# Own semaphores for the row gathers, one wait of TensorE for five rows, and buffers filled in alternating direction, in a relational graph layer

## The chip, the cores and the metric

The kernel runs on one core of a Trainium2 chip. The metric is the device time of one execution in microseconds. Three runs of the kernel before took 18,929.84, 18,938.22 and 18,953.83 us, so the median is 18,938.22 us. Lower is better.

Five engines with an instruction stream of their own take part: TensorE (PE: products, and PEld: its weight loads), VectorE (DVE), ScalarE (ACT), GpSimd (POOL) and SyncE (SP, which only issues transfers). They order their work by semaphores: an instruction can wait until a semaphore has reached a value, and can step one when it is done.

## The reference, cut to what matters

Two relational graph layers over 50,000 nodes with 128 features and 850,000 edges of 16 relations, with 8 basis matrices, then a residual and a layer norm:

```python
def _rgcn_layer(h, src, dst, rel, basis, w_comp, loop_w, bias):
    W = jnp.einsum('rb,bio->rio', w_comp, basis)
    seg = dst.astype(jnp.int32) * N_REL + rel.astype(jnp.int32)
    agg = jax.ops.segment_sum(h[src], seg, num_segments=N_ENT * N_REL)
    agg = agg.reshape(N_ENT, N_REL, -1)
    msg = jnp.einsum('nri,rio->no', agg, W)
    out = msg + h @ loop_w + bias
    return jax.nn.relu(out)

h = _rgcn_layer(x, src, dst, rel_type, basis1, w_comp1, loop_w1, bias1)
h = _rgcn_layer(h, src, dst, rel_type, basis2, w_comp2, loop_w2, bias2)
x = _layernorm(x + h, axis=-1)
```

The edges come sorted by their target `dst`. 50,000 of them are loops of a node to itself, and the kernel handles those apart; 800,000 remain.

## The kernel before

**Chunks.** The 800,000 edges are cut into rows of 128 edges, and ten rows (`K = 10`) are a chunk: 625 chunks (`C`) for each of the two layers `n`, 1,250 in all, run through by `for c in range(C)`. The two halves of a chunk have five rows each (`PER = 5`).

**Gathers.** For each row of a chunk one gather (`gather`, L198, an indirect DMA issued by GpSimd) fetches the 128 source nodes' features, 512 bytes each, from `x` or, in the second layer, from `H1`. The ten rows of a chunk land in one of six buffers (`rows[(n * C + c) % GATHERS]`, tile `g`, `GATHERS = 6`), row `k` in `g[:, k, :]`. The program text issues the gathers of chunk `c + 2` in round `c` (`FETCH = 2`). GpSimd has a stream of its own, and does nothing else in the loop but ten scatters to `FULL` (L372) and ten to `LREL` (L428) in the first layer, so it runs on ahead until a buffer is not free.

**Products of a chunk on TensorE.** For each row `k`, `pa` (L837) multiplies the gathered rows by `hot`, a matrix of 128 edges x 96 (8 bases x 12 target slots) that VectorE makes (L789) from the edges' relation weights `pm` (L615, five products for each four chunks) and their slots `own` (L782). Five products fill one bank of `pa`; then ScalarE copies it into `aT` (L844), twice for each chunk. In the next round eight products over the bases (`slots`, L689) add up `ps`, which ScalarE copies to `slots` (L693); one round later `nodes_of` spreads the slots onto nodes (`pn`, L703 and L707), adds the part of the loops (L709), applies the relu and stores `H1`, or the norm and the output.

**Loops.** `from_itself` handles the nodes' own edges, 391 tiles of 128 nodes for each layer, 0.63 for each chunk: a transpose on TensorE (L205) with its copy (L207), two products with four bases each (`hb`, L667) that VectorE weighs into `by` (L670), one with the loop matrix (L678, taken over at L679), a sum (L681) and a store to `L`.

**Order.** The instructions of TensorE and GpSimd stay in the order of the text (`manual_schedule` for these two engines); a chunk's own blocks are interleaved with steps of the generators `parts`. The other engines are put in order by the scheduler.

**Waits.** The framework adds the waits. Software-issued DMAs take eight semaphore lanes in turn, so gather `i` waits until gather `i - 8`, the last one on its lane, has landed. Each gather waits as well for the product that read its row six chunks earlier, and each of the ten products waits for its own row's lane. Every one of the ten products steps TensorE's semaphore, by one. A product steps it by more where earlier ones in the group have no step of their own: the eight products of L689 by eight at the last, the five of L615 by five.

Of the kernel before, what the change touches and what calls it, by code (L numbers as in the profile page):

```python
# [53 lines left out]
K = P // WN  # L54
# [10 lines left out]
PER = 5  # L65
Q = AT // 2
GATHERS = 6
# [9 lines left out]
def tile_rgcn_resnorm(  # L77
# [15 lines left out]
    nc = tc.nc  # L93
# [4 lines left out]
    C = -(-M // (K * P))  # L98
# [5 lines left out]
    def needed(j):  # L104

        end = min(2 * C, ROWS[j + 1] if j + 1 < len(ROWS) else 2 * C) * LIVE
        return min(NG - 1, -(-(end + LIVE) * E // (M * RUN * P)) - 1) if j else 0
# [87 lines left out]
    ps_h = ctx.enter_context(tc.tile_pool(name="ps_h", bufs=1, space=PSUM))  # L195

    def gather(to, of, idx):
        nc.gpsimd.indirect_dma_start(  # L198
            out=to, out_offset=None, in_=of, in_offset=bass.IndirectOffsetOnAxis(ap=idx, axis=0)
        )  # L200

# [13 lines left out]
    rows = [consts.tile([P, K, D], F32, name=f"g{i}") for i in range(GATHERS)]  # L215
    src = consts.tile([P, 2 * C * HALF], I32, name="src")
# [366 lines left out]
    def chunked():  # L583
        with (
# [5 lines left out]
            def at(c):  # L590
                return nc.values_load(
                    base_i[0:1, c : c + 1],
                    engines=[mybir.EngineType.SP],
                    min_val=0,
                    max_val=N - P,
                    skip_runtime_bounds_check_because="bases are clamped to N - P, and no node is below 0",
                )
# [129 lines left out]
            def asked(c):  # L727

                return min(NT, -(-(c + 1) * NT // C) + AHEAD)

            def asked_by(c):

                return min(NT, -(-asked(c) // AT) * AT) * P
# [21 lines left out]
            def later_rows():  # L755
                g = 0
                for j in range(1, len(ROWS)):
                    while g < needed(j):
                        g += 1
                        yield from runs(g, pr, lambda: asked_by(min(C - 1, now[0] + 2)))  # L760
                    yield from rows_of(j, pr)
                    ready[0] = j
                while g < NG - 1:
                    g += 1
                    yield from runs(g, pr, lambda: asked_by(min(C - 1, now[0] + 2)))

            coming = later_rows()
            ordered = ExitStack()
            ordered.enter_context(tc.manual_schedule(engines={mybir.EngineType.PE, mybir.EngineType.Pool}))
            for n, of in enumerate((x, H1)):  # L770

                kept, summed_up, multiplied, lws = None, None, None, []
                base, ks = [at(0), None, None], lambda c: min(K, -(-M // P) - c * K)
                own_parts = []

                def own_nodes(c):

                    return range(asked(c - 1) if c > 1 else 0, asked(c) if c else 0)

                def hot_of(c, pm):  # L780
                    own = hp.tile([P, K, WN], F32, name="own")
                    nc.vector.tensor_tensor(  # L782
                        own[:, : ks(c)],
                        grid[:, None, :WN].to_broadcast([P, ks(c), WN]),
                        key[:, c * K : c * K + ks(c), None].to_broadcast([P, ks(c), WN]),
                        op=OP.is_equal,
                    )
                    hot = hp.tile([P, K, NB, WN], F32, name="hot")
                    nc.vector.tensor_tensor(  # L789
                        hot[:, : ks(c)],  # L790
                        pm[:, c % Q * K : c % Q * K + ks(c), :, None].to_broadcast([P, ks(c), NB, WN]),
                        own[:, : ks(c), None, :].to_broadcast([P, ks(c), NB, WN]),
                        op=OP.mult,
                    )
                    return hot

                def loaded(n0):

                    ls = sb.tile([P, D], F32, name="ls_of")
                    nc.sync.dma_start(ls, L[n][ds(n0, P), :])  # L800
                    xw = None
                    if n:
                        xw = sb.tile([P, D], F32, name="xw")
                        nc.sync.dma_start(xw, x[ds(n0, P), :])
                    return ls, xw

                weigh = weights(0, n)
                next(weigh)
                for c in range(C):
                    now[0] = c  # L810
                    if n == 0 and c:

                        next(coming, None)
                        while ready[0] + 1 < len(ROWS) and 2 * min(C, c + FETCH + 4) > ROWS[ready[0] + 1]:
                            next(coming)
                    if c:
                        base = [at(c)] + base[:2]
                    for to in range(0 if c == 0 else c + FETCH, min(C, c + FETCH + 1)):
                        for k in range(ks(to)):
                            gather(rows[(n * C + to) % GATHERS][:, k, :], of, src[:, to * K + k : to * K + k + 1])  # L820
                    g = rows[(n * C + c) % GATHERS]
                    if c == 0:
                        if n == 0:
                            done(first_runs)
                        pm = next(weigh)
                        hot = hot_of(c, pm)
                    if c > 1:
                        kept = nodes_of(kept, c - 2, ks(c - 2), summed_up, base[2], *others, n)
                        others = loaded(base[1])
                    parts = own_parts[0] if own_parts else iter(())  # L830
                    next(parts, None)
                    aT = hp.tile([P, NB, S], F32, name="aT")
                    for k in range(0, ks(c), PER):
                        m = min(PER, ks(c) - k)
                        pa = ps_a.tile([P, BANK], F32, name="pa")
                        for i in range(m):
                            nc.tensor.matmul(  # L837
                                pa[:, i * NB * WN : (i + 1) * NB * WN],
                                g[:, k + i, :],
                                hot[:, k + i].rearrange("e b w -> e (b w)"),  # L840
                                start=True,
                                stop=True,
                            )
                        nc.scalar.copy(  # L844
                            aT[:, :, k * WN : (k + m) * WN].rearrange("d b (i w) -> d i b w", w=WN),
                            pa[:, : m * NB * WN].rearrange("d (i b w) -> d i b w", i=m, w=WN),
                        )
                        if k == 0:
                            next(parts, None)
                            if c:  # L850
                                summed_up = slots(c - 1, ks(c - 1), multiplied, n)
                            next(parts, None)
                    multiplied = aT
                    for parts in own_parts:
                        done(parts)
                    if c == 1:
                        others = loaded(base[1])
                    if c + 1 < C:
                        if (c + 1) % Q == 0:
                            pm = next(weigh)  # L860
                        hot = hot_of(c + 1, pm)
                        if c + 2 < C and (c + 2) % Q == 0:
                            weigh = weights(c + 2, n)
                            next(weigh)
                        own_parts = []
                        for i in own_nodes(c + 1):
                            own_parts.append(from_itself(i, of, n, lws))
                            if len(own_parts) == 1:
                                next(own_parts[0])
                    if n == 0 and c == 3:  # L870
                        beginning.close()
                    if n == 0 and c == C - 1:
                        done(coming)
                        count_up(pr)
                last = loaded(base[0])
                kept = nodes_of(kept, C - 2, ks(C - 2), summed_up, base[1], *others, n)
                summed_up = slots(C - 1, ks(C - 1), multiplied, n)
                nodes_of(kept, C - 1, ks(C - 1), summed_up, base[0], *last, n)
# [189 lines left out]
```

## Time and profile before

| | |
|---|---|
| median of three runs | 18,938.22 us |
| profiled execution, its own time | 18,936.72 us |
| its span, first to last instruction | 18,934.8 us |
| mean granted clock of TensorE | 0.720 of full speed |
| busy: TensorE products, weight loads | 10,703.0 us, 9,174.1 us |
| busy: GpSimd | 11,864.7 us |
| busy: VectorE, ScalarE | 6,595.5 us, 2,775.4 us |
| transfers | 1,227 MB, mean 65 GB/s |
| gathers (L198) | 12,500, some 947 ns each |
| products of L837 | 12,500, two records each (f32) |

How to read it: PE is recorded in two records for each f32 product, with PEld beside it. A line of a group names the line of the kernel, the engine, the operation, out<-in by tile names, and the count, then the busy time and the mean in ns, then the engine's idle time just before and what ended most of it. "remote" and "another core or an unknown queue" mean that the profile found no instruction that could have ended the wait. "issue" is time in which the engine waited for nothing that the profile shows. The ends of TensorE's records are modelled by the profiler, not observed. A gather's record ends when its transfer has been issued, not when the rows have landed.

### The profile page before, as it was taken

Reading aid. Unit: us, or ns where it says so; the run is one execution under the profiler, and the core shown is the slowest. Engines: PE = TensorE matmul, PEld = TensorE weight load, DVE = VectorE, ACT = ScalarE, POOL = GpSimd, SP = SyncE. Lnnn points to the kernel's source line nnn. Section 1 sums busy time; section 2 is a strip of 40 time slices with the busy share of each in tenths; the row PEclk is TensorE's granted clock in tenths of the full one; section 3 lists DMA queues with packets and bytes.
Section 4 is the critical chain, followed back from the end, with each engine's and each line's share of the span. In section 5 each row is a group of like instructions: output and inputs, shape, how many; then the busy total and the mean of one; then the engine's idle time right before and its main releaser. Section 6 shows DMA issues by size and latency. Waiting matters only on the chain.

```text
span 18934.8 us, 187693 instructions
## 1 busy us (share of the span) xinstructions
PE 10703.0 (57%) x59198; PEld 9174.1 (48%) x59198; DVE 6595.5 (35%) x14269; ACT 2775.4 (15%) x7815; POOL 11864.7 (63%) x12533
## 2 busy tenths in 40 slices
PE   4555555555555555555555555555555555555555
PEld 3444445444544445445445555445454444444445
DVE  4333334333333332333223333333333333333333
ACT  1111111111111111111111111111111111111111
POOL 5666666665666666666656666666666666666665
PEclk7777777676777776777767777777777777777777
DMA  2222222222222222222222222222222222222222
GB/s 80 69 69 65 68 66 66 66 66 63 62 62 61 61 61 61 61 61 61 61 55 66 67 66 67 66 66 67 65 66 66 66 66 66 65 66 66 66 65 62
DMA packets 1164943, 1227.02 MB, mean 65 GB/s; under 512 B 283055, under 2 KB 952401, under 8 KB 1163937
## 3 DMA queue, kind: packets, MB, share of 16 engines
q0 software_dynamic: 403552, 826.82, 16.8%
q1 hardware_dynamic: 757169, 386.65, 7.1%
q8 instruction: 472, 7.73, 0.2%
q14 instruction: 534, 4.37, 0.1%
q10 hardware_dynamic: 3216, 1.45, 0.0%
HBM read 1059.55 MB, written 154.23 MB: 64 GB/s over the span
## 4 chain that ended last, share of the span: by engine, by line
another core or an unknown queue 22%; PE 17%; issue 7%; DVE 5%; ACT 2%; DMA 0%; POOL 0%; SPq 0%; ACTq 0%; DVEq 0%; POOLq 0%
PE pa L837 6%; PE ps L689 4%; PE hb L667 4%; DVE ls L681 1%; DVE by L670 1%; DVE hot L789 1%; PE pn L703 1%; ACT aT L844 1%; PE pn L707 1%; PE po L678 0%; PE po L205 0%; DVE by L679 0%; ACT slots L693 0%; ACT sd L574 0%
## 5 line engine op out<-in xcount | busy, mean ns | idle before, releaser
L198 POOL DMA_INDIRECT g<-H,src x6250 | 5910.6, 946 | 3393.7 <-issue 1422.2
L198 POOL DMA_INDIRECT g<-in_x_dram,src x6250 | 5927.4, 948 | 3338.4 <-issue 1411.5
L837 PE MATMUL pa<-hot,g 128*128 128x96 f32 x25000 | 4125.3, 326 | 1898.8 <-DVE hot L789 1388.2
L837 PEld LDWEIGHTS pa<-hot,g 128*128 128x128 f32 x25000 | 4014.2, 243 | 2402.1 <-DVE hot L789 1434.6
L689 PEld LDWEIGHTS ps<-basis,aT 128*120 128x120 f32 x20000 | 3222.4, 240 | 927.1 <-issue 849.3
L667 PE MATMUL hb<-basis,hT 128*128 128x512 f32 x3128 | 2273.3, 818 | 2107.1 <-ACT hT L207 915.7
L689 PE MATMUL ps<-basis,aT 128*120 128x128 f32 x20000 | 3211.3, 329 | 224.3 <-issue 150.5
L670 DVE TENSOR_TENSOR by<-hb,lw 128x512 f32<-128x512 f32 x1564 | 1080.1, 691 | 6152.1 <-remote 2557.6
L789 DVE TENSOR_TENSOR hot<-pm,own 128x960 f32<-128x960 f32 x1250 | 1432.6, 1153 | 4113.1 <-remote 3585.2
L844 ACT COPY aT<-pa 128x480 f32<-128x480 f32 x2500 | 1395.2, 558 | 6619.3 <-remote 3577.7
L703 PE MATMUL pn<-slots,own 120*128 120x128 f32 x2500 | 708.5, 373 | 2448.5 <-ACT slots L693 1502.1
L703 PEld LDWEIGHTS pn<-slots,own 120*128 120x128 f32 x2500 | 470.3, 235 | 2593.2 <-ACT slots L693 1583.3
L667 PEld LDWEIGHTS hb<-basis,hT 128*128 128x128 f32 x3128 | 638.1, 253 | 2191.4 <-ACT hT L207 943.1
L681 DVE TENSOR_REDUCE ls<-by 128x128 f32<-128x1152 f32 (+1 forms) x782 | 1656.9, 2119 | 12.1
L693 ACT COPY slots<-ps 120x128 f32<-120x128 f32 x1250 | 332.4, 266 | 5771.4 <-remote 3733.1
L205 PE MATMUL po<-ident,h_own 128*128 128x128 f32 (+1 forms) x782 | 295.8, 378 | 1151.9 <-issue 399.5
L205 PEld LDWEIGHTS po<-ident,h_own 128*128 128x128 f32 (+1 forms) x782 | 138.1, 177 | 1219.9 <-issue 415.1
L707 PE MATMUL pn<-kept,shift 128*128 128x128 f32 x2496 | 604.8, 332 | 12.1 <-DVE shift L706 6.3
L615 PE MATMUL pm<-each,is_rel 128*128 128x64 f32 x3140 | 438.6, 281 | 114.4 <-issue 110.4
L707 PEld LDWEIGHTS pn<-kept,shift 128*128 128x128 f32 x2496 | 493.7, 245 | 14.2 <-DVE shift L706 7.7
L712 ACT COPY kept<-pn 128x128 f32<-128x128 f32 x1248 | 336.1, 269 | 1079.7 <-DVE a L709 603.5
L709 DVE TENSOR_TENSOR a<-pn,ls_of 128x128 f32<-128x128 f32 x1250 | 355.1, 284 | 386.6 <-remote 133.1
(148 smaller groups left out, 5082.0 us busy)
## 6 DMA issues: line engine op xcount, KB each, us to landing
g<-in_x_dram,src POOLq DMA_INDIRECT x6250
g<-H,src POOLq DMA_INDIRECT x6250
ls_of<-L SPq DMA_DIRECT2D x1250, 64.0 KB
L<-ls SPq DMA_DIRECT2D x780, 64.0 KB
H<-h SPq DMA_DIRECT2D x625, 64.0 KB
xw<-in_x_dram SPq DMA_DIRECT2D x625, 64.0 KB
out_dram<-o SPq DMA_DIRECT2D x625, 64.0 KB
h_own<-in_x_dram SPq DMA_DIRECT2D x390, 64.0 KB
```

What stands on the lines that cost most here:

```text
L198: nc.gpsimd.indirect_dma_start(out=to, out_offset=None, in_=of, in_offset=bass.IndirectOffsetOnAxis(ap=idx, axis=0))
L205: nc.tensor.transpose(tp[:, :m], h, ident[:m, :m])
L615: nc.tensor.matmul(of[:, :, j * NB : (j + 1) * NB], is_rel[:m, j * P : (j + 1) * P], EACH[n][:m], start=True, stop=True,)
L667: nc.tensor.matmul(hb[:m], hT, BASIS[n][:, b : b + few, :].rearrange("p b d -> p (b d)"), start=True, stop=True)
L670: nc.vector.tensor_tensor(by[:m, b : b + few, :], hb[:m].rearrange("p (b d) -> p b d", d=D), lw[:m, b : b + few, None].to_broadcast([m, fe ...
L681: nc.vector.tensor_reduce(ls[:m], by[:m].rearrange("p b d -> p d b"), AX.X, OP.add)
L689: nc.tensor.matmul(ps[: k * WN], aT[:, b, : k * WN], BASIS[n][:, b, :], start=b == 0, stop=b == NB - 1)
L703: nc.tensor.matmul(pn, own[: k * WN], st[: k * WN], start=True, stop=not c)
L707: nc.tensor.matmul(pn, shift, kept, start=False, stop=True)
L789: nc.vector.tensor_tensor(hot[:, : ks(c)], pm[:, c % Q * K : c % Q * K + ks(c), :, None].to_broadcast([P, ks(c), NB, WN]), own[:, : ks(c), ...
L837: nc.tensor.matmul(pa[:, i * NB * WN : (i + 1) * NB * WN], g[:, k + i, :], hot[:, k + i].rearrange("e b w -> e (b w)"), start=True, stop=True,
L844: nc.scalar.copy(aT[:, :, k * WN : (k + m) * WN].rearrange("d b (i w) -> d i b w", w=WN), pa[:, : m * NB * WN].rearrange("d (i b w) -> d i ...
```

## The change

Each half of each of the six buffers gets a semaphore of its own, `landed[0]` to `landed[11]`. Every gather steps the one of its half by 16 when it lands, instead of a lane, and the framework is told to leave these gathers' completion to it. Of a half's five products only the first waits, for the count that stands for all five rows; the others are declared free of it. A buffer is filled from row 0 to 9 in one use and from 9 to 0 in the next (`in_turn`), and the halves and rows are multiplied in the same alternating order. The framework then makes other waits of this: of a chunk's ten gathers only the first waits for TensorE, for the last product of the buffer's previous use, and gathers have no lane to wait for. As nothing waits for a single one of the five products, the last of them steps TensorE's semaphore by five. The number and the shapes of products, copies and transfers are unchanged.

```diff
     def gather(to, of, idx):
-        nc.gpsimd.indirect_dma_start(
+        return nc.gpsimd.indirect_dma_start(
@@
+            landed = [tc.alloc_semaphore(f"landed{i}") for i in range(2 * GATHERS)]
+            counts, all_of = [0] * (2 * GATHERS), {}
@@
+                def half_of(c, k):
+                    return (n * C + c) % GATHERS * 2 + k // PER, f"rows{n}_{c}_{k // PER}"
+
+                def in_turn(c, k, of=None):
+
+                    of = of or range(k)
+                    return list(of)[:: 1 - 2 * ((n * C + c) // GATHERS % 2)]
@@
-                        for k in range(ks(to)):
-                            gather(rows[(n * C + to) % GATHERS][:, k, :], of, src[:, to * K + k : to * K + k + 1])
+                        for k in in_turn(to, ks(to)):
+                            one = gather(rows[(n * C + to) % GATHERS][:, k, :], of, src[:, to * K + k : to * K + k + 1])
+                            at_h, name = half_of(to, k)
+                            counts[at_h] += 16
+                            one.then_inc(landed[at_h], 16)
+                            tc.no_tile_sem_insts.add(one.ins.name)
+                            tc.add_to_no_dep_group(name, one.ins)
+                        for k in range(0, ks(to), PER):
+                            at_h, name = half_of(to, k)
+                            all_of[name] = counts[at_h]
@@
-                    for k in range(0, ks(c), PER):
+                    halves = list(range(0, ks(c), PER))
+                    for k in in_turn(c, len(halves), halves):
                         m = min(PER, ks(c) - k)
                         pa = ps_a.tile([P, BANK], F32, name="pa")
-                        for i in range(m):
-                            nc.tensor.matmul(
+                        at_h, name = half_of(c, k)
+                        for j, i in enumerate(in_turn(c, m)):
+                            one = nc.tensor.matmul(
                                 pa[:, i * NB * WN : (i + 1) * NB * WN],
                                 g[:, k + i, :],
                                 hot[:, k + i].rearrange("e b w -> e (b w)"),
                                 start=True,
                                 stop=True,
                             )
+                            if j == 0:
+                                one.wait_op(landed[at_h], all_of[name], "sem-ge")
+                            tc.declare_no_dep(one.ins, group=name, reason="the first reader waits for all rows of the half")
+                            if j == 0:
+                                tc.declare_fence(one.ins, group=name)
@@
-                        if k == 0:
+                        if len(halves) == 1 or k == halves[in_turn(c, len(halves))[0]]:
                             next(parts, None)
```

## The prediction

> **What bounds the kernel now.** I read the page first (busy shares, costliest groups, chain), then the waits, then the timeline of single chunks. Of the page, these lines matter:
>
> ```profile
> PE 10703.0 (57%) x59198; PEld 9174.1 (48%) x59198; DVE 6595.5 (35%) x14269; ACT 2775.4 (15%) x7815; POOL 11864.7 (63%) x12533
> another core or an unknown queue 22%; PE 17%; issue 7%; DVE 5%; ACT 2%; DMA 0%; POOL 0%; SPq 0%; ACTq 0%; DVEq 0%; POOLq 0%
> L198 POOL DMA_INDIRECT g<-H,src x6250 | 5910.6, 946 | 3393.7 <-issue 1422.2
> L837 PE MATMUL pa<-hot,g 128*128 128x96 f32 x25000 | 4125.3, 326 | 1898.8 <-DVE hot L789 1388.2
> L844 ACT COPY aT<-pa 128x480 f32<-128x480 f32 x2500 | 1395.2, 558 | 6619.3 <-remote 3577.7
> ```
>
> No engine is full, and the largest share of the chain belongs to nobody that the profile can name, on a program of one core. The reader should be stopped by the last line: the copy that empties a block of five products sat idle 3,577.7 us for a "remote" releaser, although TensorE alone releases it. The timeline of one chunk shows what that is (start, duration, engine, line, what; in brackets the idle time before it):
>
> ```profile
> 8964.38 1.02 PE L667 MATMUL hb<-basis,hT 128*128 128x512 f32 x2
> 8965.24 1.25 PE L837 MATMUL pa<-hot,g 128*128 128x96 f32 x10
> 8966.32 0.41 PE L678 MATMUL po<-loop,hT 128*128 128x128 f32 x2
> 8968.29 0.69 DVE L670 TENSOR_TENSOR by<-hb,lw 128x512 f32<-128x512 f32 x1 [4.76 <-PE pn L707]
> 8972.06 0.94 POOL L198 DMA_INDIRECT g<-in_x_dram,src  x1 [0.32 <-remote]
> 8975.38 0.56 ACT L844 COPY aT<-pa 128x480 f32<-128x480 f32 x1 [8.24 <-remote]
> 8976.76 0.29 DVE L679 TENSOR_TENSOR by<-po,bias 128x128 f32<-128x128 f32 x1 [0.22 <-remote]
> 8978.95 0.29 DVE L709 TENSOR_TENSOR a<-pn,ls_of 128x128 f32<-128x128 f32 x1 [1.91 <-PE pa L837]
> 8979.86 0.94 POOL L198 DMA_INDIRECT g<-in_x_dram,src  x1 [2.10 <-PE pa L837]
> ```
>
> The five products are recorded from 8965.24 to 8966.49 (ten records, two for each f32 product), but the copy that needs them starts at 8975.38, 8.9 us later, with ScalarE idle for 8.24 us. So a recorded product is not yet a released one. The consumers' starts give the true pace of the releases: the product for L670 at 8968.29, the five of L837 7.09 us later, the one of L678 1.38 us later, the two for L709 2.19 us later. Matching every wait on TensorE with the trace's semaphore updates, 6,363 waits of VectorE and ScalarE start within 90 ns of an update; a quarter of the updates follow the recorded end by 14 to 15 ns, the median by 2.65 us, the upper quarter by 6.9 us and more. The releases of TensorE, not its recorded work, bound this kernel.
>
> SyncE and its transfers play no part: the gathers land 2.3 us after their start (median), and the copy of a block starts some 79 us after its fifth gather landed, so rows are there five chunks early. GpSimd is what is held back: it has used up its six buffers and waits for TensorE.
>
> ```profile
> POOL g L198 <- PE pa L837: 1621.8, 1277, 33.9
> POOL g L198 <- remote: 1586.1, 1153, 8.9
> 45.53 0.94 POOL L198 DMA_INDIRECT g<-in_x_dram,src  x1 [0.30 <-issue]
> ```
>
> Gathers come 1.249 us apart (0.947 busy, 0.302 gap): ten are 12.5 us, and a chunk takes 15.08 us (12,499 gaps from 44.3 to 18,892.0 us over 1,249.9 chunks). The other 2.58 us are stalls, nearly all before the first gather of a half (1,543 us in all before the first half, 1,360 before the second).
>
> **What a release costs.** In places where the releases run late and the gathers run on, the time between two releases comes in steps of 0.704 us. Medians over such places: one product of L667 with its own semaphore step 2.0 units (81 places), a pair of L703/L707 with one common step 3.0 (35), five products of L615 with one step 6.5 (16), five of L837 with five steps 10.1 (111); one of L678 is 1.0 to 2.0 (103). Products plus steps gives 2, 3, 6, 10 and 2. The program has 30,045 products and 18,798 instructions that step the semaphore, so a chunk needs 24.0 + 15.0 = 39.1 units. L615 against L837 is the row the change turns on:
>
> ```profile
> 8994.43 1.25 PE L615 MATMUL pm<-each,is_rel 128*128 128x64 f32 x10
> 9000.01 0.56 ACT L844 COPY aT<-pa 128x480 f32<-128x480 f32 x1 [4.07 <-remote]
> 9004.97 2.22 DVE L789 TENSOR_TENSOR hot<-pm,own 128x960 f32<-128x960 f32 x2 [12.51 <-remote]
> ```
>
> Here L615's five products pass in 4.96 us after the release of 9000.01; L837's took 7.09 above.
>
> The units also depend on GpSimd. Interpolated between releases, TensorE passes 4.0 units per us in the first two us after a stall of GpSimd, 2.2 after five, 1.4 after ten (one in 0.704 us); in a stall 2 per us in the first us, then up to 11 around 2 to 2.5 us. A run of ten gathers after a stall of at least 0.75 us passes 28.7 to 31.1 units (503 runs), the stall behind it 10.7 to 14.5 in 2.1 to 3.3 us.
>
> **The change part by part.** The built order of instructions is the same on every engine but for 12 rows of VectorE, ScalarE and SyncE; only waits and steps differ.
>
> - *Steps of TensorE.* Nobody waits for a single product any more, so the five steps of a block become one step of five: 18,798 instructions with a step become 8,798, and a chunk needs 24.0 + 7.0 = 31.1 units instead of 39.1. At 0.704 us that is 5.6 us where releases are saturated, which a chunk is only late in its run. In equilibrium: a run of ten passes about 29.3 units, 1.8 remain for the stall, at 2 per us 0.9 us; chunk 12.5 + 0.9 = 13.4 us. A straight line through the means instead (1.42 units per us always, and 6.9 more per us of stall: 39.1 = 1.42 x 15.08 + 6.9 x 2.58) gives 14.1 us. I take 13.6, nearer to the runs themselves, since the stall's second us, which the change does away with, is what the line's slope is made of.
> - *Waits of TensorE.* 12,500 waits for a lane become 2,500 for a half. They do not bind, rows being 79 us early. Bounds: nothing below; above, the gap between L615 (6.5) and L837 (10.1) may be theirs and not the steps', which is the same 3.6 to 4 units, counted once. Behind the first product's wait stand all of TensorE's work and, by its releases, VectorE, ScalarE and the stores on SyncE; all would wait for the fifth row instead of the first if the lead were gone: 4 x 1.25 = 5 us per half. The lead is gone only at the start of each layer: +10 us.
> - *Waits of GpSimd.* The 12,440 lane waits go, and of 12,440 waits for TensorE 1,244 stay, on the first gather of a chunk. The first eight gathers have neither wait and still stand 1.25 us apart (line of 45.53), so this is worth nothing to GpSimd; 0.017 us of each EVENT_SEMAPHORE lies in the gap. If the lane waits set the 0.30 us gap after all, up to 12,440 x 0.017 = 0.21 ms.
> - *The turn of direction.* The last product of a buffer frees the row that is filled first, so one wait covers ten gathers. It comes later than before: half a chunk. Work that hides it: five other full buffers, some 65 us of products. Two stalls per chunk become one, which is already in the run of ten.
>
> Sum: 1,250 x 13.6 = 17,000; before the first gather 44 and after the last 43; layer starts 10; 2 from the span (18,934.8) to the execution's own time (18,936.7, itself 0.01% under the median of 18,938.2). 17,100 us.
>
> [...]
>
> **Rivals.**
> 1. *GpSimd becomes the bound.* If the waits that go also slow the releases, TensorE passes 31 units within 12.5 us: 12,500 x 1.249 = 15,612, plus 320 for the 20 scatters and their stalls (L372, L428: 296 idle, 24 busy), plus 87: 16,020 us. For: the units of L837 scatter from 7 to 14, so something else takes part. Against: the saturated pace of one in 0.704 us gives 17.8 units in 12.5 us. Chance 0.2.
> 2. *Steps are not the cost, the products' passes are.* Then 39.1 units stay, and only the stalls are joined: a run of ten passes 29.3, the rest takes a stall of 2.0 us, chunk 14.5 us, 18,210 us. For: L667's 2.0 could be its two passes. Against: L615 and the L703/L707 pair lie below their ten and four. Chance 0.12.
> 3. *It changes nothing:* releases are late for a reason of the gathers alone, and stalls grow to the old length: 18,940 us. Against: the steady 1.4 units per us. Chance 0.06.
> 4. *Slower: the later wait.* If TensorE used up its lead, the wait of GpSimd for a whole chunk (half a chunk, 7.5 us, later, spread over six buffers 1.25 us per chunk) and the all-five wait would stand in the loop: 1,250 x 1.25 = +1.6 ms, 20.5 ms. It decides once the lead falls under one chunk; it is five. Chance 0.07.
>
> **How the numbers follow.** Forecast 0.55, giving 17,100 us (13.4 to 14.1 us per chunk: 16.9 to 17.7 ms). Down to rival 1 and up to rival 2 the range is 15,950 to 18,350; outside lie 3, 4 and a tail. A measurement here tells about 0.2% (38 us). Faster 0.87, same 0.06, slower 0.07.
>
> **What would show it.** Right: L198's stalls fall from 3.2 ms to about 1.4 ms and stand before first gathers only; "remote" idle time of L844 and L693 falls by a third or more; gather gaps stay 0.30 us. Rival 1: no stalls at all, and products waiting for g. Rival 2: stalls of 2 us in every chunk. The forecast is wrong if "remote" times stay while the chunk shortens, or if the gap between gathers moves.

## The result and the profile after

The changed kernel is slower: 19,693.75 us median of 4 runs (19,651.44 to 19,717.03), against 18,934.03 us (18,914.84 to 18,953.83) for the kernel before on the same chip. The ratio is 1.0399, 95% interval [1.0376, 1.0421]. The forecast was 17,100 us. The profiled execution took 19,717.03 us with a span of 19,715.2 us.

These are the page's lines of the changed kernel that answer to those shown of before: busy times, the chain, the gathers of the second layer, the five products and the copy that empties them.

```profile
PE 10883.5 (55%) x59198; PEld 9341.1 (47%) x59198; DVE 6598.9 (33%) x14269; ACT 2777.8 (14%) x7815; POOL 11886.4 (60%) x12533
another core or an unknown queue 25%; PE 17%; issue 7%; DVE 6%; ACT 1%; DVEq 0%; ACTq 0%
L198 POOL DMA_INDIRECT g<-H,src x6250 | 5921.1, 947 | 3898.4 <-issue 1761.4
L858 PE MATMUL pa<-hot,g 128*128 128x96 f32 x25000 | 4214.8, 331 | 2070.1 <-DVE hot L800 1308.5
L870 ACT COPY aT<-pa 128x480 f32<-128x480 f32 x2500 | 1384.4, 559 | 8179.5 <-remote 5265.8
```

Busy times are within 2% of before; idle times are not. The copy of L870 waits 5,265.8 us for "remote" releases where it waited 3,577.7, and the gathers of the second layer have 3,898.4 us of idle time before them where they had 3,393.7. The waits of GpSimd (waited for, us in total, times, longest) say how the stalls have changed:

```profile
POOL g L198 <- PE pa L858: 1362.9, 174, 28.0
POOL g L198 <- remote: 1229.9, 527, 10.8
POOL g L198 <- PE po L678: 1209.4, 148, 15.5
```

Fewer and longer: the two largest rows of before counted 1,277 and 1,153 waits. Nearly all stalls (913 of 969 breaks) now stand before the first gather of a chunk, as the prediction had it, and the gap between the gathers is still 0.30 us. But taking every distance between the starts of two gathers less 1.25 us, what is over 0.25 us (a break, from here on) sums to 3.98 ms, up from 3.20, not down to 1.4. A chunk takes 15.70 us; it took 15.08 us.

Sorted by length, the runs of gathers between two such breaks are 581 of ten and 280 of twenty (580 and 277 in the expectations below), where the kernel before had 517 of ten, 300 of five, 118 of fifteen and many odd ones. A run of ten with the break behind it takes 14.84 us, nearly as before (14.82). A run of twenty takes 16.72 us per ten, because a break of 8.4 us on average follows it. The timeline of core 0 shows one from its first gather to the next (start, duration, engine, line, what; in brackets the idle time before it and its releaser):

```profile
8988.82 0.95 POOL L198 DMA_INDIRECT g<-in_x_dram,src  x1 [2.18 <-remote]
...
9002.22 2.42 PE L858 MATMUL pa<-hot,g 128*128 128x96 f32 x10 [6.59 <-DVE hot L800]
...
9012.58 0.95 POOL L198 DMA_INDIRECT g<-in_x_dram,src  x1 [0.30 <-issue]
...
9017.12 0.69 DVE L670 TENSOR_TENSOR by<-hb,lw 128x512 f32<-128x512 f32 x1 [10.50 <-remote]
9017.13 0.56 ACT L870 COPY aT<-pa 128x480 f32<-128x480 f32 x1 [11.00 <-remote]
...
9019.74 2.28 PE L858 MATMUL pa<-hot,g 128*128 128x96 f32 x10
...
9022.29 0.95 POOL L198 DMA_INDIRECT g<-in_x_dram,src  x1 [8.76 <-PE pa L858]
```

Twenty gathers start from 8988.82 to 9012.58 without a break. The five products of 9002.22 are recorded as done at 9004.64, but ScalarE, which copies them, and VectorE, idle for 11.0 and 10.5 us, get their releases at 9017.1, only after GpSimd has stopped. The busy times in the three stretches (first ten gathers, second ten, the break):

```profile
core 0: us, PE busy (x) PEld busy (x) DVE busy (x) ACT busy (x) POOL busy (x), PEclk, DMA share, GB/s
8988.80:9001.30 12.50, 6.43 (x41) 6.20 (x41) 2.83 (x4) 2.11 (x6) 9.46 (x10) 0.79 0.26 68
9001.30:9013.80 12.50, 6.98 (x28) 5.53 (x28) 2.57 (x5) 0.27 (x1) 9.46 (x10) 0.64 0.22 58
9013.80:9022.30 8.50, 4.43 (x15) 3.40 (x16) 3.05 (x8) 1.34 (x5) 0.01 (x1) 0.50 0.09 25
```

TensorE starts 41 passes in the first ten gathers, 28 in the second and 15 in the break; a chunk needs 47.4 (59,198 over 1,250). Over all 280 runs of twenty the means are 50.1, 13.7 and 22.7: the first ten gathers pass a whole chunk, the second ten hardly a third of one, and the rest has to be done with GpSimd standing still. The clock column adds to it. It falls from 0.79 to 0.64 to 0.50 here, and over the first 150 runs of twenty the mean granted clock is 0.82 in the first ten, 0.60 in the second and 0.59 in the break. The block of 9019.74 takes 2.28 us, at a granted clock of 0.50 (9019.70 to 9022.10); one at 8965.24 of the kernel before took 1.25, at 1.00 (8964.90 to 8966.50). So after half a run with few passes TensorE also catches up at a lower clock; why the granted clock falls there, no run shows.

This is what the trace shows. Whether the long runs are the cause, and which part of the change makes them, is for the experiments.

### The profile page after: what moved, and what is told of

Read it like the earlier page. It is cut to its first block, busy times and chain, and to the rows that moved or that the text cites. A ratio compares the mean times of both kernels' runs of the same rounds, so it can differ in the third digit from the quotient of the medians.

```text
span 19715.2 us, 175255 instructions
## 1 busy us (share of the span) xinstructions
PE 10883.5 (55%) x59198; PEld 9341.1 (47%) x59198; DVE 6598.9 (33%) x14269; ACT 2777.8 (14%) x7815; POOL 11886.4 (60%) x12533
## 4 chain that ended last, share of the span: by engine, by line
another core or an unknown queue 25%; PE 17%; issue 7%; DVE 6%; ACT 1%; DVEq 0%; ACTq 0%
PE pa L858 6%; PE hb L667 4%; PE ps L689 3%; DVE ls L681 1%; DVE by L670 1%; DVE hot L800 1%; PE pn L703 1%; PE pn L707 1%; PE po L678 1%; PE pm L615 1%; DVE by L679 0%; ACT aT L870 0%; PE po L205 0%; DVE own L699 0%
## 5 line engine op out<-in xcount | busy, mean ns | idle before, releaser
L198 POOL DMA_INDIRECT g<-H,src x6250 | 5921.1, 947 | 3898.4 <-issue 1761.4
L858 PEld LDWEIGHTS pa<-hot,g 128*128 128x128 f32 x25000 | 4143.2, 250 | 2627.4 <-issue 2610.5
L858 PE MATMUL pa<-hot,g 128*128 128x96 f32 x25000 | 4214.8, 331 | 2070.1 <-DVE hot L800 1308.5
L667 PE MATMUL hb<-basis,hT 128*128 128x512 f32 x3128 | 2370.0, 850 | 3399.6 <-DVE by L670 2231.1
L689 PEld LDWEIGHTS ps<-basis,aT 128*120 128x120 f32 x20000 | 3275.6, 244 | 1131.9 <-issue 675.9
L689 PE MATMUL ps<-basis,aT 128*120 128x128 f32 x20000 | 3292.6, 335 | 451.3 <-ACT aT L870 430.2
L870 ACT COPY aT<-pa 128x480 f32<-128x480 f32 x2500 | 1384.4, 559 | 8179.5 <-remote 5265.8
L703 PE MATMUL pn<-slots,own 120*128 120x128 f32 x2500 | 656.7, 350 | 1422.1 <-ACT slots L693 1002.2
L703 PEld LDWEIGHTS pn<-slots,own 120*128 120x128 f32 x2500 | 452.6, 226 | 1519.9 <-ACT slots L693 1054.2
L707 PE MATMUL pn<-kept,shift 128*128 128x128 f32 x2496 | 568.6, 315 | 10.3 <-DVE shift L706 10.3
L679 DVE TENSOR_TENSOR by<-po,bias 128x128 f32<-128x128 f32 (+1 forms) x782 | 223.6, 286 | 911.0 <-remote 607.7
L207 ACT COPY hT<-po 128x128 f32<-128x128 f32 (+1 forms) x782 | 208.4, 267 | 2179.4 <-remote 1376.1
```

The lines of the kernel that those rows point to most:

```text
L198: return nc.gpsimd.indirect_dma_start(out=to, out_offset=None, in_=of, in_offset=bass.IndirectOffsetOnAxis(ap=idx, axis=0))
L667: nc.tensor.matmul(hb[:m], hT, BASIS[n][:, b : b + few, :].rearrange("p b d -> p (b d)"), start=True, stop=True)
L689: nc.tensor.matmul(ps[: k * WN], aT[:, b, : k * WN], BASIS[n][:, b, :], start=b == 0, stop=b == NB - 1)
L703: nc.tensor.matmul(pn, own[: k * WN], st[: k * WN], start=True, stop=not c)
L707: nc.tensor.matmul(pn, shift, kept, start=False, stop=True)
L858: one = nc.tensor.matmul(pa[:, i * NB * WN : (i + 1) * NB * WN], g[:, k + i, :], hot[:, k + i].rearrange("e b w -> e (b w)"), start=True, ...
```

## The experiments

Eighteen runs. One set of four, marked below, met the kernel before at 15,829 us instead of 18,934 to 19,069; each kernel is compared with the runs of the kernel before beside it.

**1. Parts of the change, one by one.** Three kernels make a table of what is kept. The first keeps the own semaphores, the one wait and the one step of five per half, but drops the turn of direction: each half is always filled from its last row and read forwards, so GpSimd waits once for each half.

```diff
-                    return list(of)[:: 1 - 2 * ((n * C + c) // GATHERS % 2)]
+                    return list(of)
-                        for k in in_turn(to, ks(to)):
+                        for k in [k for h in range(0, ks(to), PER) for k in reversed(range(h, min(h + PER, ks(to))))]:
```

> Own semaphores, one wait and one step of five per half, as in the changed kernel, but each half is always filled from its last row, so GpSimd waits for TensorE before each half (2,488 waits) and not before each chunk (1,244). Theory 1 (the change joined GpSimd's two stalls per chunk into one; gathers that run ten or twenty without a break let the pace of TensorE's releases fall to 0.6 to 1.4 units per us, so that 277 runs of twenty cost 16.7 us per ten gathers and 580 runs of ten 14.8): breaks of five come back, no run of twenty costs 16.7 us, about 14.5 us per chunk, 18,100 us (17,500 to 18,600). Theory 2 (the waits for a lane held the gathers apart, and without them they crowd out the releases): they are still gone, 19,700 us as the changed kernel. Theory 3 (the first product's wait for all five rows costs): it is still there, 19,700 us.

Measured: 18,758.42 us against 19,069.21, ratio 0.9838 [0.9822, 0.9855]. It is faster than both kernels, on the side of theory 1, though by less than that expected. Repeated in a later session, with the changed kernel beside it (expectations below): 18,755.24 us, 0.9841 [0.9824, 0.9857], the changed kernel 19,769.78 us, 1.0372 [1.0355, 1.0389].

The second only takes the turn away and fills forwards. Then each row's product has to release its row, so the single steps (18,750) and the waits of GpSimd (12,440) are back, while the semaphores and the waits of TensorE are those of the changed kernel.

```diff
-                    return list(of)[:: 1 - 2 * ((n * C + c) // GATHERS % 2)]
+                    return list(of)
```

> Own semaphores and one wait of TensorE per half as in the changed kernel, but filled and read forwards always: each gather then waits for its own row's product again (12,440 waits of GpSimd for TensorE) and each product steps the semaphore again (18,750 steps instead of 8,798). Theory 1: stalls before both halves as in the kernel before, 39.1 units per chunk as there: 18,900 us (18,700 to 19,100). If a step costs a unit of 0.7 us in late places, as the prediction had it, this is slower than the kernel with halves by 8 units per chunk, some 0.5 to 1.4 ms; if steps cost nothing, the two agree within 0.1 ms. Theory 2 and theory 3: 19,700 us or above, since lane waits are gone and the first product waits for five rows.

Measured: 19,006.62 us, 0.9965 [0.9953, 0.9976].

The third is the kernel before with the turn alone.

```diff
+                def in_turn(c, k, of=None):
+                    of = of or range(k)
+                    return list(of)[:: 1 - 2 * ((n * C + c) // GATHERS % 2)]
-                        for k in range(ks(to)):
+                        for k in in_turn(to, ks(to)):
...
-                        for i in range(m):
+                        for i in in_turn(c, m):
```

> The kernel before with nothing but the turn of direction: its lane semaphores stay, each product waits for its lane and steps the semaphore, GpSimd waits for TensorE once a chunk (1,244 waits). Theory 1: stalls are joined, runs of ten and twenty gathers as in the changed kernel, with 39.1 units per chunk to pass instead of 31.1: 19,700 us or above, up to 21,500. Theory 2: lane waits are back, 18,900 us. Theory 3: single waits are back, 18,900 us.

Measured: 19,808.78 us, 1.0390 [1.0372, 1.0407], with 723 runs of ten and 187 of twenty (17.1 us per ten) in its trace.

What follows: the turn costs 3.9% by itself, as much as the whole change; theories 2 and 3 (the missing lane waits, the wait for all five rows) fall, since the first kernel has both of these and no turn, and is the fastest of them all. The steps: the first two differ by 9,952 steps of TensorE and as many waits of GpSimd, and by (0.9965 - 0.9838) x 19,069 = 242 us, 24 ns for a step and a wait together. They also differ in the order in which a half is filled and in where the breaks fall, so 24 ns isn't the price of a step by itself. With the turn the steps are worth nothing that shows (1.0390 with them, 1.0399 without).

The waits of GpSimd in the trace of the first kernel:

```profile
POOL g L198 <- remote: 2037.7, 790, 12.0
POOL g L198 <- PE pa L858: 555.5, 147, 31.0
```

The breaks are back: 190 runs of five, 643 of ten, 268 of fifteen, none of twenty; breaks sum to 3.04 ms. Of these, breaks over 4 us are 0.71 ms, in the changed kernel 2.73 ms.

**2. Are the gathers to blame at all?** Two kernels leave gathers out, so that products read old rows and only their time says something, both in the session with the kernel before at 15,829 us.

```diff
+                        if to >= GATHERS:
+                            continue
                         for k in in_turn(to, ks(to)):
...
```

> The changed kernel without its gathers but for the first six chunks of each layer (the products then read old rows; the output is not the reference's). Theory 1 (gathers in flight slow TensorE's releases): no late releases are left; the products, loads and VectorE alone remain, 11,000 to 14,500 us (TensorE is busy 10,884 us in the changed kernel's profile). If TensorE is late for a reason of its own, the time stays above 17,000 us.

Measured: 8,968.73 us (one run), below what was expected.

```diff
-                        for k in in_turn(to, ks(to)):
+                        for k in in_turn(to, ks(to))[:: 1 if to < GATHERS else 2]:
```

> The changed kernel with every second gather left out after the first six chunks of each layer (the output is not the reference's): runs of five, 6.25 us, per chunk, one stall per chunk. Theory 1: a run of five passes 15 of a chunk's 31.1 units, the stall of 4 to 5.5 us the rest: 10.5 to 12 us per chunk, 13,100 to 15,000 us. If the pace of the releases were TensorE's own and not tied to the gathers: above 17,000 us, with longer stalls.

Measured: 8,980.72 us (one run), far below either expectation: half the gathers cost TensorE nothing there. The same kernel again, in a session with the kernel before at 19,044 us:

> The kernel with every second gather left out (output not the reference's) once more. With the kernel before at 15.8 ms: 8,980 us as before, TensorE 90% busy. With the kernel before at 19 ms: 13,100 to 15,000 us if gathers in flight slow the releases as theory 1 has it, above 17,000 us if the releases are late for a reason of TensorE's own, 9,000 us if dense runs alone do it.

Measured: 11,071.50 us (one run). Below what theory 1 expected, far below 17,000. The busy lines, the kernel without gathers first, then the two profiles of the one with half of them:

```profile
PE 8109.9 (90%) x59198; PEld 7176.2 (80%) x59198; DVE 6564.1 (73%) x14269; ACT 2797.7 (31%) x7815; POOL 142.2 (2%) x153
```

```profile
PE 8108.9 (90%) x59198; PEld 7177.8 (80%) x59198; DVE 6579.3 (73%) x14269; ACT 2803.6 (31%) x7815; POOL 6032.7 (67%) x6343
```

```profile
PE 8927.2 (81%) x59198; PEld 7748.6 (70%) x59198; DVE 6549.8 (59%) x14269; ACT 2747.8 (25%) x7815; POOL 6017.7 (54%) x6343
```

In the second profile TensorE's updates (the steps of its semaphore as the trace has them) follow the recorded ends by 14 to 15 ns, up to the 99th percentile. In the third, the same program, the median is 15 ns too, but a quarter comes some 2 us late or more and one in a hundred 6 us or more. So with releases on time the work without gathers takes 9.0 ms, TensorE 90% busy. Late releases are a condition that one session did not have and the others had; the same chip had given 19,069 us earlier. Where it exists, half the gathers take far less time than all of them (11,072 us against 19,799 in that session), so the lateness goes with the gathers; the kernel without any wasn't run there. What differs between the sessions the profile doesn't name: the transfers took the same time (the gathers' queue 16.8% of 8,979 us and 13.6% of 11,070 us, 1,508 and 1,505 us).

**3. Gathers further apart.** A small GpSimd write behind each gather.

```diff
+            pause = consts.tile([P, 1], F32, name="pause")
...
                             tc.add_to_no_dep_group(name, one.ins)
+                            if c:
+                                nc.gpsimd.memset(pause, 0.0)
```

> The changed kernel with a small GpSimd write (one element per partition, 0.10 to 0.13 us in the rows of constants) behind each gather after the first chunk, so that gathers stand some 1.4 us apart instead of 1.25. Theory 1, if the pace of the releases falls because gathers come faster than whatever carries both can take: the releases keep up, stalls nearly vanish, 14.0 to 14.6 us per chunk, 17,600 to 18,300 us. If the pace falls with each gather whatever its distance: the pauses add up to 1.5 us per chunk of ten and only replace part of the stalls, 19,700 to 20,500 us.

Measured: 19,521.89 us, 1.0237 [1.0220, 1.0254]. The edit didn't space anything, as the timeline shows:

```profile
9000.92 0.94 POOL L198 DMA_INDIRECT g<-in_x_dram,src  x1 [0.19 <-issue]
9001.85 0.12 POOL L839 MEMSET pause<- 128x1 f32 x1
9002.16 0.95 POOL L198 DMA_INDIRECT g<-in_x_dram,src  x1 [0.19 <-issue]
```

The write lies in the gap that was there anyway, and gathers are still 1.25 us apart. That it is some 1.5% below the changed kernel, with 125 runs of twenty instead of 280, isn't explained; the two later profiles of the changed kernel (below) have 220 and 198 of them at the same ratio to the kernel before, 1.040 and 1.037, and runs of ten at 15.07 and 15.17 us instead of 14.84, so the number of runs of twenty doesn't set the time by itself. With two writes (`for _ in range(2 if c else 0)`) the distance is 1.365 us:

> The changed kernel with two small GpSimd writes behind each gather instead of the one that hid in the 0.30 us gap: 0.946 + 2 x 0.118 + 0.19 and a little make a gather every 1.4 us or so, 14.0 us for ten. If the pace of the releases falls because the gathers come too densely (theory 1, queue): stalls shrink to under 0.6 us per chunk, no runs of twenty with stalls of 8 us, 17,700 to 18,400 us. If any gather in flight costs the same whatever its distance, the stalls of 2.1 us and more per chunk stay: 19,900 to 20,600 us.

> The same with three small writes: a gather every 1.52 us, 15.2 us for ten. Theory 1, queue: no stalls, GpSimd sets the time, 19,100 to 19,400 us. If stalls stay at 2.1 us and more per chunk: 21,300 us or above.

Measured in the session with the kernel before at 15,829 us: 17,452.95 us (1.1025 [1.1007, 1.1043]) and, with three writes, 19,392.41 us (one run). Both are GpSimd's own time, 12,500 x 1.365 = 17.06 ms and 12,500 x 1.522 = 19.0 ms, and 0.4 ms for the start, the scatters and the end; the chain of the first reads

```profile
POOL 62%; issue 11%; PE 5%; DMA 2%; DVE 0%; ACT 0%; SPq 0%; POOLq 0%; DVEq 0%; ACTq 0%
```

and the same sum fits the kernel before there: 15.61 ms at 1.249 us, of 15.83. Since neither says anything of late releases, the changed kernel and the one with two writes were run again:

> The changed kernel itself once more, since the kernel before took 15,829 us beside the last four runs and 18,934 to 19,069 us beside the others. If the kernel before takes some 15.8 ms here again, TensorE's releases are on time and GpSimd's 12,500 gathers at 1.25 us set the end: the changed kernel then takes 15,600 to 15,900 us and is within 1% of it. If the kernel before takes some 19 ms, the changed one takes 3.5 to 4.5% more.

> The kernel with two small GpSimd writes behind each gather (a gather every 1.365 us) once more, beside the changed kernel. With the kernel before at 15.8 ms: 17,450 us as before. With the kernel before at 19 ms: if releases fall behind because the gathers come too densely, stalls go and it takes 17,450 to 18,400 us, less than either; if every gather slows the releases whatever its distance, stalls of 2.1 us and more per chunk stay and it takes 19,900 to 20,600 us.

Measured, with the kernel before at 19,043.92 us: the changed kernel 19,798.75 us, 1.0399 [1.0382, 1.0416]; with two writes 19,063.58 us, 1.0009 [0.9998, 1.0020]. Spacing takes 3.7% off the changed kernel although it gives GpSimd 1.4 ms more to do, but less than expected: breaks fall from 4.05 to 2.17 ms, not to nothing. Its trace still has 180 runs of twenty, but with gathers 0.11 us further apart they take 15.4 us per ten instead of 16.7 to 17.0.

**4. The lack of breaks by itself.** Nothing of the change is undone here; fourteen small writes to `pause` (2.2 us) stand behind every ten gathers.

```diff
                             tc.add_to_no_dep_group(name, one.ins)
+                        for _ in range(14 if c else 0):
+                            nc.gpsimd.memset(pause, 0.0)
```

> The changed kernel with fourteen small GpSimd writes (0.156 us each by the runs with two and three of them, 2.2 us in all) behind every ten gathers and nothing else: no two chunks are gathered without a break. Theory 1 (what costs is that gathers of two chunks run on without a break: 218 to 277 runs of twenty at 16.7 to 17.0 us per ten, against 14.8 to 15.0 for runs of ten): the runs of twenty end, a chunk takes 14.7 to 15.0 us, 18,500 to 18,800 us, 5 to 6.5% less than the changed kernel beside it, though GpSimd has 2.7 ms more to do. If long runs are only a sign of something else, the pause adds to the stalls or replaces them: the changed kernel's time or more. (In a session in which the kernel before takes 15.8 ms the pause adds 2.7 ms and shows nothing.)

> The changed kernel beside these. Kernel before at 19 ms: 1.038 to 1.042 of it. Kernel before at 15.8 ms: 15,600 to 15,900 us, within 1% of it.

> The kernel with a wait before each half beside these. Kernel before at 19 ms: 0.982 to 0.986 of it. Kernel before at 15.8 ms: within 1% of it, since GpSimd sets the end of both.

Measured: 18,606.45 us, 0.9764 [0.9748, 0.9780], the fastest complete kernel where releases are late; the changed kernel beside it 19,769.78 us and the one with waits per half 18,755.24 (given under 1). A pause takes 5.9% off. The timeline of one break, and two rows of the gathers' waits: the largest with no known releaser and the largest on TensorE:

```profile
9020.34 0.94 POOL L198 DMA_INDIRECT g<-in_x_dram,src  x1 [0.30 <-issue]
...
9021.27 2.15 POOL L839 MEMSET pause<- 128x1 f32 x14
...
9023.55 0.56 ACT L873 COPY aT<-pa 128x480 f32<-128x480 f32 x1 [3.39 <-remote]
...
9023.79 0.94 POOL L198 DMA_INDIRECT g<-in_x_dram,src  x1 [0.37 <-remote]
```

```profile
POOL g L198 <- remote: 275.9, 682, 1.0
...
POOL g L198 <- PE pn L707: 32.0, 87, 0.6
```

Of 1,286 runs 1,206 are of ten, a chunk takes 14.82 us, and GpSimd hardly waits for TensorE any more, though nothing but its own pause was added. Releases still come late there: the copy of a block starts 3.6 us (median) after the recorded end of the block's last product, in the changed kernel 2.0. It is the latest that go, one in a hundred 10.7 us against 21.1. So the turn costs its time by the gaps that GpSimd no longer makes: turn, waits and steps are all still there, and a gap of its own ends the loss. That the gap must be more than a mere break, the next experiment shows. The same pause wasn't run in a kernel without the turn, so how much of the 5.9% is the turn's loss taken back and how much a gain of its own stays open. The kernel with two waits and spaced gathers, to see whether the remedies add up:

> The kernel with a wait before each half and one step of five per half (1.6% faster than the kernel before), with two small GpSimd writes behind each gather (a gather every 1.365 us, which took 3.7% off the changed kernel). If both gains are gains in the pace of the releases under gathers, part of the second adds to the first: 18,300 to 18,700 us. If the breaks do all that the pacing can do, the pacing only lengthens the runs: 18,800 to 19,300 us.

Measured: 18,823.90 us, 0.9880 [0.9863, 0.9896], slightly worse than the waits per half alone. They don't add up.

**5. How long must a break be?** The same edit with seven writes (1.1 us) and ten (1.56 us) per ten gathers, and with seven behind each five.

```diff
-                        for _ in range(14 if c else 0):
+                        for _ in range(7 if c else 0):
```

> As the kernel with a pause of fourteen small writes behind every ten gathers, but with seven: 1.1 us instead of 2.2. Drain theory (the releases come in a burst only some 2 us after the last gather was issued: 8.2 units per us from 2.0 to 2.5 us in the trace with fourteen, 1.3 to 1.8 before that): 1.1 us end before the burst, TensorE falls behind, stalls of 2 us and runs of twenty come back, 18,800 to 19,700 us. If any break counts by its length, the pause of 2.2 us was longer than needed (GpSimd waited for TensorE only 275.9 us by the largest row there): 12.5 + 1.1 and some 0.3 us of waits, 17,300 to 17,800 us.

```diff
-                        for k in in_turn(to, ks(to)):
+                        for j, k in enumerate(in_turn(to, ks(to))):
...
+                            for _ in range(7 if c and j % PER == PER - 1 else 0):
+                                nc.gpsimd.memset(pause, 0.0)
```

> The same fourteen writes per ten gathers, seven behind each five: two breaks of 1.1 us in place of one of 2.2. Drain theory: neither reaches the burst, 19,000 to 19,800 us, clearly more than the kernel with one break of 2.2 us (0.976 of the kernel before). If length alone counts: the same as with one break, 18,600 us.

> Ten small writes behind every ten gathers, 1.56 us. Drain theory: too short for the burst by half a microsecond, 18,700 to 19,500 us. If length alone counts: 12.5 + 1.56 and some 0.2 us of waits, 17,800 to 18,000 us.

Measured: 1.1 us per ten 19,475.58 us, 1.0217 [1.0200, 1.0234]; 1.56 us 19,040.25 us, 0.9988 [0.9977, 1.0000]; twice 1.1 us 18,637.47 us, 0.9771 [0.9755, 0.9787]. The drain theory has the two single pauses right and the split one wrong, length alone the other way round, so neither holds. Two breaks of 1.1 us do as well as one of 2.2, so a break need not last the some 2 us that the drain theory named (in that trace some 1.7 units, products plus steps as in the prediction, pass per us in the first us after the last gather, and 2.3 in the first two us of the next run). But a shorter sum doesn't make a shorter chunk: the pause of 1.1 us ends every run at ten gathers and takes only some 1.5% off the changed kernel. So neither the length of the break nor the mere end of a run is all of it. The breaks in the traces (all, pauses included, and those over 4 us):

| kernel | chunk, us | breaks, ms | over 4 us, ms |
|---|---|---|---|
| changed | 15.70 | 3.98 | 2.73 |
| pause 1.1 us per ten | 15.47 | 3.70 | 1.81 |
| pause 1.56 us per ten | 15.15 | 3.29 | 0.98 |
| before | 15.08 | 3.20 | 0.72 |
| waits per half | 14.95 | 3.04 | 0.71 |
| twice 1.1 us | 14.85 | 2.93 | 0.27 |
| pause 2.2 us per ten | 14.82 | 2.90 | 0.24 |

The rest of the breaks grows from 1.25 to 2.66 ms down the table, the long ones shrink faster. A reading that the table fits but doesn't prove: TensorE needs some 2.2 us per chunk without gathers. If GpSimd gives them evenly, that is all it costs; what it doesn't give comes back as waits, in the changed kernel in lumps of 8 us, after a stretch in which few releases passed and the clock had dropped. No shorter sum than 2.2 us was found that holds the pace; between 1.56 and 2.2 us nothing was tried.

## Why the prediction was wrong

- *What bounds the kernel.* Right for the sessions with late releases: half the gathers take 11.1 ms there, and a pause of GpSimd, which only adds to its work, makes the kernel faster. Rival 1's GpSimd bound of 16,020 us exists, but the kernel before reached it (15,829 us) in the one session where releases were on time; the change isn't what it takes. What the changed kernel does there wasn't measured.
- *The step that failed: the turn of direction, costed at nothing.* "Two stalls per chunk become one, which is already in the run of ten." It isn't: in 280 cases the next chunk's wait was already met when its gather came up (0.30 us of idle time before the eleventh gather of a run of twenty), and twenty gathers went out without a break. The prediction looked for the work that hides the wait (five full buffers) and found it; it didn't ask what the wait did while it lasted. Price: 19,769.78 - 18,755.24 = 1,015 us, 5.4%, between the changed kernel and the one with waits per half; the turn alone, put into the kernel before, costs 3.9%.
- *The term that was mis-sized: steps of TensorE, costed at 0.704 us in late places.* By rival 2's own sum, 18,210 us without it, it carried 1.1 of the 1.8 ms of forecast gain. The steps came to 24 ns each, a wait of GpSimd included, in the pair without the turn, and nothing in the pair with it. The units of a block were no price of its contents: in the changed kernel's trace L615's block, which wasn't touched, went from a median of 6.5 units to 11.0 (88 places), the L703/L707 pair from 3.0 to 5.0, while L858's block fell from 10.1 to 7.1. So something beside the contents sets them; that it is how long the gathers had been running fits the slowing pace within a run, but wasn't shown block by block. By the same interpolation a run of ten passes 25.4 units, not 29.3, once the ones for steps are left out.
- *Waits of TensorE and GpSimd: nothing.* Right, as far as waits are counted: the kernel with own semaphores and single steps is within 0.35% of the kernel before, the gap stays 0.30 us, and in the changed kernel's waits TensorE waits for rows of g three times, 16 us.
- *Rival 4, slower.* The right side for the wrong reason. Its condition, a lead of under one chunk, never came; the three waits for rows say that the lead held.
- *The signs.* Two of the prediction's own signs spoke against it: stalls at 3.98 ms where 1.4 was named, and "remote" idle time up by 47% (3,577.7 to 5,265.8 us) where a third less was named. That stalls stand before first gathers only was nearly met, and meant nothing for the time.

## What to carry to other kernels

A wait that holds back a producer may be what lets its neighbours run; before removing or joining waits, look at what the other engines get done while they last. A price fitted to places where everything is late measures how late it is there, so check it on a block that the change doesn't touch, or against a pair that differs in that item alone. Here the largest gain was a deliberate pause: GpSimd given 2.7 ms more to do made the kernel 5.9% faster than the changed one and 2.4% faster than before. That holds where releases are late; in the session where they were on time the two writes behind each gather made it 10% slower than before.

## What the runs showed of the hardware that was not expected

- TensorE's releases trailed its records by many us while gathers ran (median some 3 us, one in ten over 9 us in the changed kernel's second profile, among the updates that the trace has: 7,684 for 8,798 steps), and in another session not at all: the kernel with half the gathers took 8,981 us there (8,738 updates for 8,798 steps) and 11,072 us where releases were late. The profile names no cause. The pace fell while gathers ran without a break: interpolated, in the changed kernel, some 3.8 units per us just after a break, 1.2 after 12 us, 0.6 to 0.7 after 15 us.
- An indirect gather of 0.95 us left a gap of 0.30 us before the next, in which another GpSimd instruction of 0.12 us was free (gathers 1.25 us apart with it and without); two made the distance 1.365 us, three 1.522 us.
- The mean clock granted to TensorE went with how busy it was: 0.952 at 90% busy (no gathers, and half of them where releases were on time), 0.885 at 81% (half of them where releases were late), 0.717 at 55% (the changed kernel).
